# The head of a two-layer kernel: the first four weight chunks arrive in nine transfers of whole rows, and the idle matmuls at the start are lengthened

## The chip, the core and the metric

The kernel runs on one core of a Trainium2 chip. The metric is device time in microseconds for one execution, the median over the runs. A separate execution was recorded by the hardware profiler; all readings of single instructions, waits and transfers are from that one.

## The reference

Eight batches of 256 tokens with 1024 features pass two layers, each with a residual:

```python
# layer 0: per batch b a mask of zeros and ones and one number coeff[b]
sign = 2 * mask - 1
x = x + x @ W0.T + b0 + coeff[b] * (x @ sign[b])
# layer 1: a dense weight and a low-rank adapter chosen by itok[b]
x = x + x @ W1.T + b1 + 2.0 * ((x @ A[itok[b]]) @ B[itok[b]])
```

All of it is in float32, the mask is int32. In the first layer the weight of batch b is W0.T + coeff[b] * (2 * mask[b] - 1), so each batch has a weight of its own, made on the chip from a mask of 4 MB.

## The kernel before

Features lie on the 128 partitions; tokens run along the free dimension. Batch 0 goes through its weight in eight chunks of 128 input features by 1024 outputs (`first_batch`, L300); batches 1 and 2 in pieces of 256 inputs by 512 outputs (`first_layer`, L269); batches 3 to 7 use a scheme with seven instead of eight block products (class `Seven`, L335). After four batches the second layer of that group follows, also with seven products at two levels (`second_layer`, L702). Then the other four batches run the same way.

A piece of weight is made in two steps (`build`, L228). ScalarE turns the int32 mask into 2c * mask - c in float32 (L243; c is the batch's coefficient, held in `two_c` and `neg_c`). VectorE adds W0 to it (L251). TensorE then multiplies (L309 for batch 0, L284 for batches 1 and 2). One float32 matmul instruction of 256 columns appears as two passes in the records. From piece 8 on the identity has been added to W0 once (L236), which gives the residual; in batch 0 it is added while the sums leave PSUM (L322).

Loads are issued on SyncE's queue (SP) in the order of the pieces, four ahead of the piece that TensorE is at (`load`, L179; `load_to`). A transfer is issued when its buffer is free and the semaphore it uses has been served by its earlier user; eight such semaphores go round. W0 stays in one tile, `w0_sb`, for all batches; its chunks arrive with batch 0. For the first four chunks mask and W0 come in halves of 128x512 (256 KB each, L203), stored so that a half is contiguous in memory: mask half, W0 half, mask half, W0 half. The very first half is converted in two quarters of 256 outputs (`parts`, L152). x of chunk 0 is issued by ScalarE's queue (L205), x of chunk 1 by SP (L207), x of chunks 2 and 3 by SP (L209).

At the start, while the first bytes are on the way, TensorE multiplies zeros into a bank that nobody reads (`idle`, L98): 256 columns, then the little matmul `c_ps` that spreads the eight coefficients over the partitions (L106, it waits for the row of coefficients), then 256, 256 and 128 columns. VectorE makes `two_c` and `neg_c` from `c_ps` (L110, L112).

The order of instructions on each engine is made by a scheduler from the order of the program; `behind(...)` and `issue_after` pin some of them after others. The functions that the diff touches:

Of the kernel before, what the change touches and what calls it, by code (L numbers as in the profile page):

```python
# [9 lines left out]
F32 = mybir.dt.float32  # L10
I32 = mybir.dt.int32
AF = mybir.ActivationFunctionType
ALU = mybir.AluOpType

P = 128
OH = 512
CG = 2
OQ = 256
BY_HALF = 4
SEVEN = (3, 4, 5, 6, 7)  # L20
SCALING = 2.0

# [2 lines left out]
def kernel(  # L25
# [10 lines left out]
    b1: bass.AP,  # L36
    lora_a: bass.AP,
    lora_b: bass.AP,
    outT: bass.AP,
):  # L40

# [22 lines left out]
    nc = tc.nc  # L64
    B, NG, _, _, T = xT.shape
# [32 lines left out]
    def idle(*columns: int):  # L98
        for n in columns:
            nc.tensor.matmul(  # L100
                idle_ps[:, :n], lhsT=zeros[:, :P], rhs=zeros[:, :n], start=True, stop=True
            )

    idle(T)
    c_ps = psum.tile([P, B], F32, tag="ps", name="c_ps")
    spread = nc.tensor.matmul(c_ps, lhsT=one_row, rhs=c_row, start=True, stop=True)  # L106
    with tc.issue_after(spread.ins):
        idle(T, T, T // 2)
    two_c = const.tile([P, B], F32, tag="two_c", name="two_c")
    nc.vector.tensor_scalar_mul(two_c, c_ps, 2.0)  # L110
    neg_c = const.tile([P, B], F32, tag="neg_c", name="neg_c")
# [27 lines left out]
    anchors = {}  # L139
# [6 lines left out]
    def behind(what: str):  # L146
        return tc.issue_after(anchors[what].ins) if what in anchors else nullcontext()

    def pair(name):
        return qpool.tile([P, 2, CG, OQ], F32, tag="q", name=name)  # L150

    def parts(k: int):  # L152

        every = slice(0, OH)
        if k == 0:
            quarters = [(slice(0, 1), slice(q * OQ, (q + 1) * OQ)) for q in range(2)]
            return quarters + [(slice(1, 2), every)]
        return [(slice(i, i + 1), every) for i in range(2)] if k < BY_HALF else [(slice(0, 2), every)]

    def part(a, i: int):  # L160

        flat = a.rearrange("p i f -> (p i f)")
        return flat.rearrange("(i p f) -> i p f", i=2, p=P)[i]
# [15 lines left out]
    def load(k: int):  # L179

        b, h, g = pieces[k]

        if b in SEVEN and k % (2 * NG) >= 6 and b >= GB:
            pool, tag = qpool, "q"
        elif b in SEVEN and b % 2 and k % (2 * NG) < 6:
            pool, tag = tpool, "T"
        else:
            pool, tag = wpool, "w"  # L190
        weff[k] = pool.tile([P, CG, OH], F32, tag=tag, name=f"w_{k}")
        last = (k + 1) % (GB * 2 * NG) == 0
        pairs = [(weff[k].bitcast(I32), mask[b, g if b == 0 else h * NG + g])]
        if b == 0:
            pairs.append((w0_of(k), w0T[g]))
        x_pair = g // CG if b == 0 and g % CG == 0 else g if h == 0 else None
        if x_pair is not None:
            x = x_sb[b, x_pair] = xpool.tile([P, CG, T], F32, tag=f"x{x_pair}", name=f"x_{b}_{x_pair}")
        if k < BY_HALF:

            for i in range(2):
                for t, a in pairs:
                    nc.sync.dma_start(t[:, i], part(a, i))  # L203
                if k == 0 and i == 0:
# [12 lines left out]
        if k == NG:  # L217
            nc.sync.dma_start(b0_sb, b0)
        if k == 2 * NG:
            nc.sync.dma_start(itok_sb, itok)  # L220
        for n, (q, r) in enumerate(W1_ORDER):
            if k == 0 and r % 2 == 0:
                two = pair(f"w1_{q}_{r // 2}")
                raw[q, r], raw[q, r + 1] = two[:, 0], two[:, 1]
            if k == 2 * NG + 2 * n // 3:
                nc.sync.dma_start(raw[q, r], w1T[q, r])

    def build(k: int):  # L228
# [8 lines left out]
        w = weff[k]  # L237
        m = w.bitcast(I32)
        for i, o in parts(k):


            with behind("bias"):
                nc.scalar.activation(  # L243
                    w[:, i, o],
                    m[:, i, o],
                    AF.Identity,
                    bias=neg_c[:, b : b + 1],
                    scale=two_c[:, b : b + 1],
                )
            with behind("adds"):  # L250
                weff_at[k] = nc.vector.tensor_add(w[:, i, o], w[:, i, o], w0_of(k)[:, i, o])  # L251
            anchors["weights"] = weff_at[k]

    loaded = 0

# [44 lines left out]
    def first_batch(y, beside):  # L300

        ps = [bank(f"ps1_0_{i}") for i in range(NC // 2)]
        for c in range(NC):
            load_to(c + LOADS_AHEAD + 1)
            build(c + BUILDS_AHEAD)
            w = weff.pop(c)
            for ot in range(NC):
                h, j = divmod(ot, TPH)
                nc.tensor.matmul(  # L309
                    ps[ot // 2][:, ot % 2, :],  # L310
                    lhsT=w[:, h, j * P : (j + 1) * P],
                    rhs=x_sb[0, c // CG][:, c % CG, :],
                    start=c == 0 and ot % 2 == 0,
                    stop=c == NC - 1,
                    skip_group_check=True,
                )
# [826 lines left out]
```

## Time and profile before

| | us |
|---|---|
| median of 3 runs | 407.4 (407.25 to 407.57) |
| the profiled execution's own time | 407.66 |
| its span, first to last instruction | 406.0 |
| TensorE busy in the span | 401.6 |
| VectorE busy | 314.2 |
| ScalarE busy | 137.1 |
| first mask half landed | 3.52 |
| first W0 half landed | 4.74 |
| first matmul of batch 0 | 5.35 |
| first matmul of batch 1 | 34.83 |
| first matmul of batch 3 | 90.09 |

All times inside the profile count from the span's start. PE is TensorE's matmuls and PEld its weight loads, DVE VectorE, ACT ScalarE, POOL GpSimd, SP SyncE. The slices of the page cut the span into 40 equal parts of 10.15 us; a digit is the busy share in tenths. In a row of stretches the numbers are the stretch, its length, busy time and (in brackets) instructions of each engine, the granted clock, the share of the DMA engines and GB/s. A line of the chain of waits is start, duration and what ran. A row of the timeline is start, duration, engine, line of the kernel, instruction, its tiles and shapes, how many, and in square brackets the idle time before it with what ended it. A matmul's record is longer than the distance to the next one, since matmuls overlap; their rate is read from the distance between starts.

### The profile page before, as it was taken

How to read it: one execution, taken by the hardware profiler on the slowest of the kernel's cores; microseconds unless marked ns; L12 is line 12 of the kernel's file. 1: busy time of each engine (PE TensorE's matmuls, PEld its weight loads, DVE VectorE, ACT ScalarE, POOL GpSimd, SP SyncE). 2: the span in 40 equal slices, each digit the busy share in tenths (PEclk: the TensorE clock that was granted, in tenths of full speed). 3: DMA queues.
4: the chain of work that ended last, by engine and by line, in shares of the span. 5: the costliest groups of instructions: out<-in, count | busy, mean ns of one | idle time of the engine just before them, and what ended most of it. 6: DMA issues, size and time to landing. Idle time of an engine off the chain costs nothing.

```text
span 406.0 us, 6808 instructions
## 1 busy us (share of the span) xinstructions
PE 401.6 (99%) x2562; PEld 360.0 (89%) x2562; DVE 314.2 (77%) x451; ACT 137.1 (34%) x223; POOL 52.5 (13%) x103
## 2 busy tenths in 40 slices
PE   8999999999999999999999999999999999999997
PEld 6888888889977888888899999999998788888886
DVE  2447696979992779987999999999926247898595
ACT  4444535673114213132141927528221420102200
POOL 0000143004944221011040000400000000000000
PEclk9999999999999999999999999999999999999999
DMA  8999999990699799766998947631022237555654
GB/s 286 399 403 396 401 409 417 391 366 5 215 364 353 243 342 320 237 231 210 313 383 317 345 148 289 223 109 54 27 79 68 78 127 241 170 152 155 212 173 158
DMA packets 41700, 99.56 MB, mean 245 GB/s; under 512 B 5700, under 2 KB 6340, under 8 KB 41668
## 3 DMA queue, kind: packets, MB, share of 16 engines
q1 hardware_dynamic: 32978, 76.11, 53.8%
q0 software_dynamic: 6240, 18.90, 12.3%
q10 hardware_dynamic: 2450, 4.13, 2.8%
q8 instruction: 20, 0.33, 0.3%
q14 instruction: 12, 0.10, 0.1%
HBM read 79.19 MB, written 19.92 MB: 244 GB/s over the span
## 4 chain that ended last, share of the span: by engine, by line
PE 90%; DVE 7%; DMA 1%; ACT 1%; issue 0%; SPq 0%; DVEq 0%; ACTq 0%
PE X L727 23%; PE ps L284 14%; PE X L427 13%; PE Z L727 12%; PE ps L309 7%; PE Z L427 6%; PE Y L727 6%; PE Y L427 4%; DVE w L251 3%; PE G L745 2%; DVE s L363 2%; PE psh L762 2%; DVE t L380 1%; PE W L868 1%; DMA w_sb<-w0T 1%; DVE y L453 1%
## 5 line engine op out<-in xcount | busy, mean ns | idle before, releaser
L243 ACT ACTIVATE w<-w,neg_c,two_c 128x1024 f32<-128x1024 int32 (+2 forms) x69 | 79.1, 1183 | 60.4 <-DMA w<-mask 50.4
L251 DVE TENSOR_TENSOR w<-w,w_sb 128x1024 f32<-128x1024 f32 (+2 forms) x69 | 77.7, 1142 | 27.0 <-ACT w L243 19.8
L284 PE MATMUL ps<-x,w 128*128 128x256 f32 x256 | 55.4, 379 | 0.0
L284 PEld LDWEIGHTS ps<-x,w 128*128 128x128 f32 x256 | 48.6, 190 | 6.6
L446 ACT ACTIVATE y<-X,b_sb 128x128 f32<-128x128 f32 x60 | 17.2, 368 | 69.9 <-PE X L427 69.9
L427 PE MATMUL X<-t,s 128*128 128x128 f32 x288 | 34.1, 276 | 0.0
L883 DVE TENSOR_TENSOR c<-c,e 128x512 f32<-128x512 f32 x48 | 31.8, 682 | 1.8 <-ACT c L755 1.8
L427 PEld LDWEIGHTS X<-t,s 128*128 128x128 f32 x288 | 33.0, 192 | 0.2
L309 PE MATMUL ps<-x,w 128*128 128x256 f32 x128 | 29.5, 394 | 0.2 <-DVE w L251 0.2
L755 ACT COPY c<-G 128x512 f32<-128x512 f32 x32 | 16.4, 600 | 38.8 <-PE G L745 38.8
L309 PEld LDWEIGHTS ps<-x,w 128*128 128x128 f32 x128 | 25.3, 199 | 4.2 <-DVE w L251 0.5
L783 ACT COPY e<-X 128x512 f32<-128x512 f32 x16 | 9.4, 587 | 48.6 <-PE X L727 48.6
L785 DVE TENSOR_TENSOR c<-X,c 128x512 f32<-128x512 f32 x24 | 16.3, 686 | 8.9 <-PE X L727 8.7
L427 PE MATMUL X<-t,w 128*128 128x128 f32 x192 | 22.5, 276 | 0.4 <-DVE y L453 0.4
L727 PE MATMUL X<-T_t,l_S_s 128*128 128x256 f32 x96 | 22.7, 379 | 0.0
L427 PEld LDWEIGHTS X<-t,w 128*128 128x128 f32 x192 | 21.9, 192 | 0.5 <-DVE y L453 0.5
L363 DVE TENSOR_TENSOR s<-w,w 128x1024 f32<-128x1024 f32 x18 | 21.7, 1217 | 0.1
L727 PEld LDWEIGHTS X<-T_t,l_S_s 128*128 128x128 f32 x96 | 18.2, 190 | 2.5
L785 DVE TENSOR_TENSOR e<-Y,e 128x512 f32<-128x512 f32 x8 | 5.5, 691 | 17.6 <-PE Y L727 17.6
L427 PE MATMUL Z<-t,s 128*128 128x128 f32 x160 | 18.8, 275 | 0.0
L427 PE MATMUL X<-x,w 128*128 128x128 f32 x160 | 18.8, 275 | 0.0
L427 PE MATMUL Y<-x,w 128*128 128x128 f32 x160 | 18.7, 275 | 0.0
(145 smaller groups left out, 672.0 us busy)
## 6 DMA issues: line engine op xcount, KB each, us to landing
w<-mask SPq DMA_DIRECT2D x60, 512.0 KB, 7.0
l_S_s<-leaf_S_s SPq DMA_DIRECT2D x32, 256.0 KB, 2.7
x<-xT SPq DMA_DIRECT2D x31, 256.0 KB, 6.6
l_A_s<-leaf_A_s SPq DMA_DIRECT2D x24, 256.0 KB, 2.8
l_S_a<-leaf_S_a SPq DMA_DIRECT2D x24, 256.0 KB, 3.2
w<-w1T SPq DMA_DIRECT2D x16, 256.0 KB, 7.2
outT<-c POOLq DMA_DIRECT2D x15, 256.0 KB, 5.5
outT<-c ACTq DMA_DIRECT2D x15, 256.0 KB, 2.4
```

The costliest lines, as they stand in the source:

```text
L243: nc.scalar.activation(w[:, i, o], m[:, i, o], AF.Identity, bias=neg_c[:, b : b + 1], scale=two_c[:, b : b + 1],)
L251: weff_at[k] = nc.vector.tensor_add(w[:, i, o], w[:, i, o], w0_of(k)[:, i, o])
L284: nc.tensor.matmul(ps[j // 2][:, j % 2, :], lhsT=w[:, c, j * P : (j + 1) * P], rhs=x_sb[b, g][:, c, :],  start=first and j % 2 == 0, stop= ...
L309: nc.tensor.matmul(ps[ot // 2][:, ot % 2, :], lhsT=w[:, h, j * P : (j + 1) * P], rhs=x_sb[0, c // CG][:, c % CG, :], start=c == 0 and ot % ...
L363: anchors["weights"] = anchors["sums"] = op(s, self.w[x, a], self.w[y, a])
L427: anchors["products"] = nc.tensor.matmul(ps[:, j, :], lhsT=w[:, c, j * P : (j + 1) * P], rhs=r, start=first and a == 0 and c == 0 and j == ...
L446: sent = nc.scalar.activation(self.out(i, v)[:, j, :], ps[:, j, :], AF.Identity, bias=b0_sb[:, ot : ot + 1])
L727: anchors["inner"] = nc.tensor.matmul(ps[:, j, :], lhsT=l[:, c, j * P : (j + 1) * P], rhs=r[:, c, :], start=first and c == 0 and j == 0, s ...
L755: nc.scalar.copy(dest[b // 2][u, b % 2], ps[b])
L783: anchors["copies"] = nc.scalar.copy(out, ps)
L785: own["reads"] = anchors["reads"] = nc.vector.tensor_add(out, ps, other)
L883: nc.vector.tensor_add(o, o, x)
```

## The change

Three things change together.

First, for chunks 0 to 3 of batch 0, mask and W0 no longer come as separate transfers into their tiles. The host lays out a new array `head`: for each of nine parts, a row per feature that holds the mask's outputs, then W0's outputs, and in the first part also x of chunk 0 (256 tokens). The parts are outputs 0 to 256, 256 to 512 and 512 to 1024 of chunk 0, and two halves of each of chunks 1, 2 and 3. Each part is one transfer, a row of 3 KB (first), 2 KB (second) or 4 KB (the rest) for each partition, into a tile borrowed from buffers that are used later: the tiles T, t and q. x of chunk 0 is read from there; ScalarE's queue no longer issues it.

Second, for these chunks ScalarE reads the mask from the head tile and writes into the weight tile, and VectorE adds W0 from the head tile. W0 reaches `w0_sb` later: ScalarE copies it there (nine copies, `put_w0`), the copies of chunk c placed behind the conversion of piece c + 4.

Third, zeros on TensorE: 128 more columns ahead of `c_ps` and 64 more at the end.

```diff
-BY_HALF = 4
+HEAD = [(0, 0, 256, True), (0, 256, 512, False), (0, 512, 1024, False)]
+HEAD += [(c, h * OH, (h + 1) * OH, False) for c in range(1, 4) for h in range(2)]
+N_HEAD = 4
...
-    idle(T)
+    idle(T, T // 2)
...
-        idle(T, T, T // 2)
+        idle(T, T, T // 2, T // 4)
...
+    in_head = {}
+    row = 0
+    for c, a, e, with_x in HEAD:
+        n = 2 * (e - a) + (T if with_x else 0)
+        if n > 2 * OQ:
+            pool, tag = (tpool, "T") if c + 1 < N_HEAD else (qpool, "q")
+        else:
+            pool, tag = spool, "t"
+        t = pool.tile([P, n], I32, tag=tag, name=f"head_{c}_{a}")
+        in_head.setdefault(c, []).append((a, e, t, head[row * P : (row + n) * P]))
+        row += n
+
     def parts(k: int):
...
+        if k not in in_head:
+            return [(weff[k], weff[k].bitcast(I32), w0_of(k))]
+        w = weff[k].rearrange("p i o -> p (i o)")
+        return [
+            (w[:, a:e], t[:, : e - a], t[:, e - a : 2 * (e - a)].bitcast(F32))
+            for a, e, t, _ in in_head[k]
+        ]
+
+    def x_of(c: int):
+
+        if c:
+            return x_sb[0, c // CG][:, c % CG, :]
+        return in_head[0][0][2][:, -T:].bitcast(F32)
+
+    def put_w0(c: int):
+
+        for a, e, t, _ in in_head[c]:
+            nc.scalar.copy(w0_sb[:, c, a:e], t[:, e - a : 2 * (e - a)].bitcast(F32))
...
-        if k < BY_HALF:
-
-            for i in range(2):
-                for t, a in pairs:
-                    nc.sync.dma_start(t[:, i], part(a, i))
-                if k == 0 and i == 0:
-                    nc.scalar.dma_start(x[:, 0], part(xT[0, 0], 0))
-                elif k == 0:
-                    nc.sync.dma_start(x[:, 1], part(xT[0, 0], 1))
-                elif x_pair is not None and i == 0:
-                    nc.sync.dma_start(x, xT[b, x_pair])
+        if k in in_head:
+            for _, _, t, at in in_head[k]:
+                nc.sync.dma_start(t, at.rearrange("(p f) -> p f", p=P))
+            if k == 0:
+                nc.sync.dma_start(x[:, 1], xT[0, 0][:, 1])
+            elif x_pair is not None:
+                nc.sync.dma_start(x, xT[b, x_pair])
...
-            with behind("bias"):
-                nc.scalar.activation(
-                    w[:, i, o],
-                    m[:, i, o],
-                    AF.Identity,
-                    bias=neg_c[:, b : b + 1],
-                    scale=two_c[:, b : b + 1],
+            with behind("bias" if b else "first"):
+                anchors["first"] = nc.scalar.activation(
+                    w, m, AF.Identity, bias=neg_c[:, b : b + 1], scale=two_c[:, b : b + 1]
                 )
             with behind("adds"):
-                weff_at[k] = nc.vector.tensor_add(w[:, i, o], w[:, i, o], w0_of(k)[:, i, o])
+                weff_at[k] = nc.vector.tensor_add(w, w, w0)
             anchors["weights"] = weff_at[k]
+        if N_HEAD <= k < 2 * N_HEAD:
+            with behind("first"):
+                put_w0(k - N_HEAD)
...
-                    rhs=x_sb[0, c // CG][:, c % CG, :],
+                    rhs=x_of(c),
...
-                    x_sb[0, ot // CG][:, ot % CG, :],
+                    x_of(ot),
```

x of chunks 2 and 3 is now issued behind both halves of chunk 2, where it stood between them. The conversions of batch 0 are pinned in their order, each after the one before.

More of the change, by code (lines that the diff above doesn't have):

```diff
@@ L38 @@
     lora_b: bass.AP,
+    head: bass.AP,
     outT: bass.AP,
@@ L150, in pair @@
         return qpool.tile([P, 2, CG, OQ], F32, tag="q", name=name)
-    def parts(k: int):
[L154 to L163, printed above, removed]
+    in_head = {}
[9 more added lines that the diff above has]
+        row += n
+    def parts(k: int):
+        if k not in in_head:
[12 more added lines that the diff above has]
+            nc.scalar.copy(w0_sb[:, c, a:e], t[:, e - a : 2 * (e - a)].bitcast(F32))
     def w0_of(k: int):
@@ L236, in build @@
                     nc.vector.tensor_add(d, d, ident)
-        w = weff[k]
-        m = w.bitcast(I32)
-        for i, o in parts(k):
-            with behind("bias"):
-                nc.scalar.activation(
-                    w[:, i, o],
-                    m[:, i, o],
-                    AF.Identity,
-                    bias=neg_c[:, b : b + 1],
-                    scale=two_c[:, b : b + 1],
+        for w, m, w0 in parts(k):
+            with behind("bias" if b else "first"):
+                anchors["first"] = nc.scalar.activation(
+                    w, m, AF.Identity, bias=neg_c[:, b : b + 1], scale=two_c[:, b : b + 1]
                 )
             with behind("adds"):
-                weff_at[k] = nc.vector.tensor_add(w[:, i, o], w[:, i, o], w0_of(k)[:, i, o])
+                weff_at[k] = nc.vector.tensor_add(w, w, w0)
             anchors["weights"] = weff_at[k]
+        if N_HEAD <= k < 2 * N_HEAD:
+            with behind("first"):
+                put_w0(k - N_HEAD)
     loaded = 0
@@ L1121 @@
     }
-    def by_part(a):
-        a[:] = np.moveaxis(a, 1, 0).reshape(a.shape)
     arrays["mask"][0] = np.asarray(mask_Bx4096x4096_ik1)[0].reshape(D // P, P, 2, OH)
-    for k in range(BY_HALF):
-        by_part(arrays["mask"][0, k])
-        by_part(arrays["w0T"][k])
-    by_part(arrays["xT"][0, 0])
+    w0T, x0 = np.asarray(L0_cond_W).T, x[0].T
+    rows = []
+    for c, a, e, with_x in HEAD:
+        i = slice(c * P, (c + 1) * P)
+        row = [np.asarray(mask_Bx4096x4096_ik1)[0, i, a:e], laid(w0T[i, a:e]).view(np.int32)]
+        if with_x:
+            row.append(laid(x0[i]).view(np.int32))
+        rows.append(np.concatenate(row, axis=1).reshape(-1))
+    arrays["head"] = np.concatenate(rows)
     nc = bacc.Bacc("TRN2", target_bir_lowering=False, num_devices=1)
```

## The prediction

> **What bounds the kernel now.** I read the page first: engine shares and slices.
>
> ```profile
> PE 401.6 (99%) x2562; PEld 360.0 (89%) x2562; DVE 314.2 (77%) x451; ACT 137.1 (34%) x223; POOL 52.5 (13%) x103
> PE   8999999999999999999999999999999999999997
> DMA  8999999990699799766998947631022237555654
> GB/s 286 399 403 396 401 409 417 391 366 5 215 364 353 243 342 320 237 231 210 313 383 317 345 148 289 223 109 54 27 79 68 78 127 241 170 152 155 212 173 158
> ```
>
> TensorE is busy everywhere but at the two ends, and for the first 90 us (nine slices) the DMA engines are full as well, near 400 GB/s. So two things can pace that stage. Next, the chain of waits in order of time:
>
> ```profile
> 1.31 3.43 DMA w_sb<-w0T
> 4.87 0.43 DVE w L251
> 5.35 29.48 PE ps L309 x128
> 34.83 55.25 PE ps L284 x256
> 90.09 3.57 PE X L427 x32
> 93.66 3.57 PE Y L427 x32
> 97.23 3.73 PE X L427 x32
> ```
>
> Until 5.35 us the kernel waits for W0's first half; from there TensorE runs without a break. But 128 matmul passes in 29.48 us are slow: 256 like passes take 55.25 us (216 ns each), so 128 should take 27.6. Busy time in stretches of 2 us shows where the 1.85 us are:
>
> ```profile
> 4.00:6.00 2.00, 1.82 (x6) 1.26 (x6) 0.76 (x2) 1.18 (x3) 0.00 (x0) 1.00 0.91 324
> 6.00:8.00 2.00, 2.00 (x6) 1.60 (x5) 0.69 (x1) 0.37 (x2) 0.00 (x0) 1.00 1.05 394
> 8.00:10.00 2.00, 2.00 (x9) 1.67 (x8) 0.69 (x1) 1.48 (x2) 0.00 (x0) 1.00 1.04 376
> 10.00:12.00 2.00, 2.00 (x11) 1.75 (x10) 1.19 (x2) 0.93 (x2) 0.00 (x0) 1.00 1.03 394
> ```
>
> The third number is TensorE's, its records in brackets. In the records passes start 427 ns apart up to 8.50 us and 216 ns apart afterwards, and the trace's clock record begins full speed at 8.60 us. The first eight passes are at half speed.
>
> The last row of the chain holds 3.73 us where its neighbours hold 3.57. The timeline says why:
>
> ```profile
> 86.61 5.17 ACT L243 ACTIVATE w<-w,neg_c,two_c 128x1024 f32<-128x1024 int32 x4 [0.71 <-DMA w<-mask]
> 87.89 2.50 DVE L251 TENSOR_TENSOR w<-w,w_sb 128x1024 f32<-128x1024 f32 x2 [0.72 <-ACT w L243]
> 97.63 1.22 DVE L363 TENSOR_TENSOR s<-s,w 128x1024 f32<-128x1024 f32 x1
> ```
>
> ScalarE waits for a mask of batch 3 until 86.61; VectorE then works without idle from 87.89 to 98.85, and the matmuls that read this sum go on at 98.91, 0.06 us late. TensorE thus has no slack there against a chain that starts with a landing of the full DMA stream. Starting TensorE earlier pays only as far as that landing moves too.
>
> [...]full speed lasts from 8.60 to 407.96 us, 399.36 us[...]. [...]W0's second half lands on its engines between 5.65 and 6.94, fifteen of them by 6.32. [...]x of chunk 0 from ScalarE's queue shares those engines; its 128 packets lie among SP's from 3.2 to 4.3 us.
>
> **The change, part by part.**
>
> *Zeros.* Before, zeros stream to 1.89, the coefficient row arrives, its spread streams at 2.32, zeros again 2.84 to 4.97, and the first real pass, its weights loaded from 5.35, streams at 5.52. The added 128 columns (two passes of 213 ns) run 1.89 to 2.31, just up to the spread, so two_c and neg_c stay at 2.78 and 2.86. The added 64 columns (two of 107 ns) run 4.97 to 5.18. [...]
>
> *First transfer.* Packets of 1, 2 and 4 KB take 46, 84 and 159 ns, so 3 KB takes some 121 (estimate). Each engine carries 8 rows: 8 x 121 = 0.97 us where the first mask took 0.67 and landed at 3.52. So mask, W0 and x land together at 3.82; before, W0 was there at 4.74 and x at 4.94. Then ScalarE 0.59, VectorE 0.42 and 0.2 of hand-overs: weights at 5.03. The zeros end at 5.18; real passes stream from there, 0.33 earlier than before, weights loaded beneath the last zeros.
>
> *What mask and W0 in one row costs.* Before, ScalarE converted a mask while its W0 was still in flight; now both steps follow the landing: 0.02 + 0.81 + 0.04 + 0.69 + 0.05 = 1.61 us (the times of chunk 1 before) where W0's landing was followed by 0.88. At full clock the first two quarters need 8 x 216 ns, to 6.93. The second quarter (landing about 4.5) is ready by 5.6, in time. The third transfer, 1152 KB into the stream, is nominally there at 5.8; the same byte was there at 6.94 before, with one engine 0.62 behind the rest. I take 6.0, so ready at 7.6 (7.4 to 8.5). TensorE idles 0.7 us, and begins the second half of chunk 0 at 7.6 instead of 8.77: 1.15 us ahead. Chunk 1 follows with 1.33 us per half against 1.73 on TensorE; x of chunks 2 and 3 (landed at 13.34, needed at 12.8) and chunk 4 (weights 0.94 us ahead before) are tight unless the stream moves too.
>
> *DMA stream.* 256 KB in rows of 2 KB took 0.667 us per landing, 512 KB in rows of 4 KB 1.28. Seven transfers of 512 KB save 7 x 0.054 = 0.38 us, the first two and x 0.07 (1.71 against 1.64 on an engine). The engines also lost about 0.75 us by 8 us (1928 KB where full rate would have moved them by 7.0), half of it at 4.2 to 5.8, and the slowest 0.6 more. With ScalarE's transfer gone and twice the bytes behind each issue I take 0.3 of that back, bounds 0 and 0.8. Sum 0.75 us (0.45 to 1.25). Total bytes are unchanged. SP's issues fall from 18 to 11 for these chunks; at 0.33 to 0.47 us each they aren't what the engines wait for later.
>
> *W0 put in place.* Nine copies on ScalarE, 0.6 us for 512 columns (its 128x512 COPY row, from PSUM there), 0.4 for 256: 5.0 us between 18 and 30 us, 1.2 to 1.4 behind each conversion of chunks 4 to 7. ScalarE's idle times there are 2.07, 1.39, 2.63 and 1.33 us, so they fit; without that cover a conversion comes up to 0.1 late, where weights stand 1 us ahead of TensorE. VectorE's additions of the identity wait for the last copy, at about 30; their readers start at 34.8. The buffers that the head borrows are next wanted after 50 us. Two ScalarE conversions of chunks around batch 3 swap places, and VectorE takes them in the same order as before. All nothing.
>
> *Sum.* TensorE comes 1.15 us earlier to the point at 98.9, the landing behind VectorE's chain 0.75: the smaller counts. Later stages follow from TensorE's own results. Profiled execution: 407.66 (span 406.0 and 1.66 around it) - 0.75 = 406.9. It was 0.26 above the median of the runs, so 406.65.
>
> **Rivals.**
>
> *More (406.2).* The engine that fell 0.62 behind doesn't, and the stream gains 1.2. For: one packet of 608 ns at 4.74 stands alone. Against: such stalls may strike anywhere.
>
> *The stream is no faster (407.2).* Larger rows save bus time, but landings are set by the slowest engine; at 80 to 90 us it trails the first by 2 us, and the head's saving can drown in that. Then TensorE arrives early and waits at 98.9; 0.0 to 0.4 is left, 407.2. The early start is then hidden anyway.
>
> *The clock isn't raised earlier (407.2).* [...]Real passes then start 0.33 earlier at half clock, eight of them end at 8.6, 0.17 ahead of before, plus the 0.06 of the wait at 98.9: 0.23.
>
> *Slower (408.8).* TensorE's new idle time between 6.93 and the third transfer's weights is its own danger. [...]1.8 us lost, start equivalent to 10.2 against 8.77, 1.4 later, all of it on the path.[...]
>
> **How the numbers follow.** Main case 0.45 at 406.65 (406.3 to 406.9); more 0.17; no faster stream 0.14; clock as before 0.12; slower 0.12. 0.2% (about what a measurement here can tell from no change) is 0.81 us, so under 406.6: half of the main case and "more", 0.40. Over 408.2: 0.12. Between: 0.48. The range runs from a stream gain of 1.6 (the bounds of rows and losses, and some of the slow engine's) to the hidden cases with the spread of runs: 405.8 to 407.7, with the slower case left out.
>
> **What would show it.** Passes 216 ns apart from the first real one; first conversion at about 3.9, first pass near 5.2; a hole in TensorE from 6.9 to 7.6; the mask wait at 86.61 moved to about 85.9; a wait for VectorE of some 0.4 us inside the row at 97.23. It is wrong if passes stay at 427 ns to 8.6, if they return to it after 8.6, or if that mask wait hasn't moved or moved by more than 1.3.

## The result and the profile after

The kernel after takes 407.83 us (median of 22 runs, 407.48 to 408.25); the kernel before took 407.25 us in the same session (22 runs, 406.79 to 407.92). The ratio is 1.0015, 95% interval 1.0009 to 1.0022. So it is a little slower, by some 0.6 us, where 406.65 was forecast, some 0.75 us faster; 407.83 lies above the range of 405.8 to 407.7. The change is small, but its interval leaves out 1, and it has the other sign than forecast. The two profiled executions differ by less than the medians do (407.83 after, 407.66 before); why one pair is a weak measure here comes out of the experiments.

The page of the kernel after, first the engines' shares, then TensorE and the DMA engines in 40 slices:

```profile
PE 401.7 (99%) x2566; PEld 360.6 (89%) x2566; DVE 314.1 (77%) x451; ACT 141.7 (35%) x232; POOL 52.6 (13%) x103
PE   8999999999999999999999999999999999999997
...
DMA  7999999990699799776898947631122247545654
GB/s 272 407 403 396 395 406 417 413 360 4 223 365 337 250 335 318 244 231 217 296 372 338 345 148 278 235 111 52 27 78 57 80 140 233 170 153 161 211 167 160
```

ScalarE has 4.6 us more work, the nine copies. The first slice, up to 10.15 us, moved 272 GB/s where it was 286 before. That is 0.14 MB less in just the stretch that the change was to speed up. In the second slice the stream is a little faster (407 against 399); from the third to the seventh the two are within 5 GB/s.

The longest pieces of the chain of waits, in order of time, start and duration (the conversion and addition between the first two rows are left out):

```profile
1.78 5.59 DMA head<-head
...
8.99 26.17 PE ps L328 x120
35.16 55.25 PE ps L303 x256
...
93.98 3.57 PE Y L446 x32
97.55 3.57 PE X L446 x32
```

Before, the chain began with W0's first half and TensorE had no break after 5.35 us. Now its first long piece is the third transfer, issued at 1.78 and landed at 7.37, and the first eight passes have dropped off the chain: the 120 passes after them are what counts, and these begin at 8.99, 1.62 us after the landing. They run at full speed (218 ns each) and bring batch 1 to 35.16, where it began at 34.83. The row at 97.55 no longer holds a wait for VectorE.

The stretches of 2 us, columns as before (the third number is TensorE, in brackets its records; the last two are the DMA engines' share and GB/s):

```profile
4.00:6.00 2.00, 2.00 (x8) 1.82 (x7) 0.85 (x2) 1.11 (x2) 0.00 (x0) 1.00 0.82 255
6.00:8.00 2.00, 2.00 (x6) 1.55 (x6) 0.00 (x0) 0.61 (x1) 0.00 (x0) 1.00 0.95 341
8.00:10.00 2.00, 1.67 (x9) 1.14 (x8) 0.82 (x2) 1.03 (x2) 0.00 (x0) 1.00 1.03 420
10.00:12.00 2.00, 2.00 (x11) 1.76 (x10) 1.25 (x2) 1.23 (x2) 0.00 (x0) 1.00 1.01 410
```

Two things stand in the last column. From 4 to 8 us the engines moved 255 and 341 GB/s, against 324 and 394 before; from 8 us on they moved 420 and 410, against 376 and 394. The loss comes first, in the stretch that decides when the second half of chunk 0 is there; the gain comes behind it.

The timeline of the start (start, duration, engine, line, instruction, tiles, in square brackets the idle time before it and what ended it):

```profile
3.90 0.60 ACT L263 ACTIVATE w<-head,neg_c,two_c 128x256 f32<-128x256 int32 x1 [0.99 <-DMA head<-head]
...
4.54 0.43 DVE L267 TENSOR_TENSOR w<-w,head 128x256 f32<-128x256 f32 x1 [1.22 <-ACT w L263]
4.74 0.60 ACT L263 ACTIVATE w<-head,neg_c,two_c 128x256 f32<-128x256 int32 x1 [0.24 <-DMA head<-head]
...
5.58 3.08 PE L328 MATMUL ps<-head,w 128*128 128x256 f32 x8
...
7.39 0.82 ACT L263 ACTIVATE w<-head,neg_c,two_c 128x512 f32<-128x512 int32 x1 [2.05 <-DMA head<-head]
...
8.24 0.69 DVE L267 TENSOR_TENSOR w<-w,head 128x512 f32<-128x512 f32 x1 [2.44 <-ACT w L263]
...
8.99 1.35 PE L328 MATMUL ps<-head,w 128*128 128x256 f32 x5 [0.33 <-DVE w L267]
```

The first weights stand at 4.97, 0.33 us ahead of before (5.30). TensorE is still at its zeros and takes its first real pass at 5.58, where it took it at 5.35. Then ScalarE waits 2.05 us for the third part, VectorE 2.44 for ScalarE, and TensorE gets the second half of chunk 0 at 8.99.

At batch 3, the same view:

```profile
86.41 5.09 ACT L263 ACTIVATE w<-w,neg_c,two_c 128x1024 f32<-128x1024 int32 x4 [0.71 <-DMA w<-mask]
87.68 2.44 DVE L267 TENSOR_TENSOR w<-w,w_sb 128x1024 f32<-128x1024 f32 x2 [0.73 <-ACT w L263]
...
97.37 1.23 DVE L382 TENSOR_TENSOR s<-s,w 128x1024 f32<-128x1024 f32 x1
97.39 3.74 PE L446 MATMUL X<-t,s 128*128 128x128 f32 x32
```

The mask that was there at 86.61 is there at 86.41: the whole stream gained 0.20 us. VectorE's sum ends at 98.60, where it ended at 98.85. TensorE comes to that point later than before (the block begins at 97.39, in the kernel before at 97.07), so it finds the sum ready. That hides half of the loss in this pair: batch 1 begins 0.33 us later than before, the row at 97.55 is 0.16 us shorter than its counterpart, and the two executions differ by 0.17 us.

### The profile page after: what moved, and what is told of

It reads as the page before. It is cut to its first block, busy times and chain, and to the rows that moved or that the text cites. A ratio compares the mean times of both kernels' runs of the same rounds, so it can differ in the third digit from the quotient of the medians.

```text
span 406.1 us, 6825 instructions
## 1 busy us (share of the span) xinstructions
PE 401.7 (99%) x2566; PEld 360.6 (89%) x2566; DVE 314.1 (77%) x451; ACT 141.7 (35%) x232; POOL 52.6 (13%) x103
## 4 chain that ended last, share of the span: by engine, by line
PE 89%; DVE 7%; DMA 1%; ACT 1%; issue 0%; SPq 0%; DVEq 0%; ACTq 0%
PE X L746 23%; PE ps L303 14%; PE X L446 13%; PE Z L746 12%; PE ps L328 6%; PE Z L446 6%; PE Y L746 6%; PE Y L446 4%; DVE w L267 3%; PE G L764 2%; DVE s L382 2%; PE psh L781 2%; DMA head<-head 1%; DVE t L399 1%; PE W L887 1%; DVE y L472 1%
## 5 line engine op out<-in xcount | busy, mean ns | idle before, releaser
L263 ACT ACTIVATE w<-w,neg_c,two_c 128x1024 f32<-128x1024 int32 x60 | 72.5, 1248 | 49.4 <-DMA w<-mask 44.3
L267 DVE TENSOR_TENSOR w<-w,w_sb 128x1024 f32<-128x1024 f32 x60 | 72.1, 1220 | 18.0 <-ACT w L263 14.7
L303 PE MATMUL ps<-x,w 128*128 128x256 f32 x256 | 55.4, 379 | 0.0
L303 PEld LDWEIGHTS ps<-x,w 128*128 128x128 f32 x256 | 48.6, 190 | 6.6
L328 PE MATMUL ps<-x,w 128*128 128x256 f32 x112 | 24.3, 379 | 0.0
L328 PEld LDWEIGHTS ps<-x,w 128*128 128x128 f32 x112 | 21.3, 190 | 2.9
```

What stands on the lines that cost most here:

```text
L263: anchors["first"] = nc.scalar.activation(w, m, AF.Identity, bias=neg_c[:, b : b + 1], scale=two_c[:, b : b + 1])
L267: weff_at[k] = nc.vector.tensor_add(w, w, w0)
L303: nc.tensor.matmul(ps[j // 2][:, j % 2, :], lhsT=w[:, c, j * P : (j + 1) * P], rhs=x_sb[b, g][:, c, :],  start=first and j % 2 == 0, stop= ...
L328: nc.tensor.matmul(ps[ot // 2][:, ot % 2, :], lhsT=w[:, h, j * P : (j + 1) * P], rhs=x_of(c), start=c == 0 and ot % 2 == 0, stop=c == NC - ...
```

## The experiments

My theory after the result: **supply**. The second half of chunk 0 and chunk 1 come later than before, since the stream of the head is slower in the first 8 us and since ScalarE must wait for mask and W0 both; that pins TensorE near 9 us whenever its clock would have let it be there earlier. Rivals: the new **zeros** delay the coefficients and the first pass; the **copies** on ScalarE hold something up; a **clock** that falls back in the hole.

All times are medians; the kernel before stood at 407.3 us in every session (407.25 to 407.32). Each ratio is to the kernel before. Each profile is one execution, which may lie well off its kernel's median.

### Zeros alone, and the change without its zeros

The kernel before with the two new zeros:

```diff
-    idle(T)
+    idle(T, T // 2)
...
-        idle(T, T, T // 2)
+        idle(T, T, T // 2, T // 4)
```

> The kernel before with the longer zeros alone. If the late third transfer is what costs (supply), the zeros are harmless or help: two_c and neg_c come 0.3 us later, still ahead of the first mask at 3.5; [...]TensorE then waits only for the second half's weights (ready at 7.8 in the profile before): 0.0 to 0.5 us faster than before. If the zeros themselves cost (they push the first real pass, or the coefficients), 0.3 to 0.6 us slower, as much as the whole change.

Measured: 407.07 us, ratio 0.9993 (0.9986 to 0.9999). The zeros cost nothing; they may have won a little. This is the lowest median of all kernels here and the only one whose interval lies below 1.

The kernel after with the zeros of before (the same edit backwards):

> The changed kernel with the zeros of before. Supply: the second half of chunk 0 is still ready only near 8.9, so the time stays within 0.2 us of the changed kernel (0.4 to 0.7 slower than before). Zeros at fault: back to before, within 0.2 us.

Measured: 407.83 us, ratio 1.0014 (1.0005 to 1.0023), just as with the new zeros. Its profiled execution had the clock at full speed from 6.23 us on, the earliest so far, and didn't profit from it. The timeline:

```profile
5.16 2.51 PE L328 MATMUL ps<-head,w 128*128 128x256 f32 x8
7.42 0.82 ACT L263 ACTIVATE w<-head,neg_c,two_c 128x512 f32<-128x512 int32 x1 [2.25 <-DMA head<-head]
8.27 0.69 DVE L267 TENSOR_TENSOR w<-w,head 128x512 f32<-128x512 f32 x1 [2.64 <-ACT w L263]
9.02 1.16 PEld L328 LDWEIGHTS ps<-head,w 128*128 128x128 f32 x6 [1.75 <-DVE w L267]
```

The eight passes began 0.42 us earlier than in the kernel after and were half of the time at full speed, and yet the second half of chunk 0 begins at 9.02 against 8.99. What went ahead of it has been waited away: the weight loads stood still for 1.75 us. So zeros neither cause the loss nor can they cure it. Nor did the clock fall back in the hole: TensorE was idle for 1.35 us ahead of 9.02, and the 120 passes from there took 26.17 us, 218 ns each.

### Other transfers

The kernel after, with each part of 512 outputs sent as two transfers, first the mask's half of the row, then W0's:

```diff
-                nc.sync.dma_start(t, at.rearrange("(p f) -> p f", p=P))
+                rows = at.rearrange("(p f) -> p f", p=P)
+                cut = t.shape[1] // 2 if t.shape[1] == 2 * OH else t.shape[1]
+                nc.sync.dma_start(t[:, :cut], rows[:, :cut])
+                if cut < t.shape[1]:
+                    nc.sync.dma_start(t[:, cut:], rows[:, cut:])
```

> The changed kernel, but every part of 512 outputs is sent as two transfers, mask then W0, cut from the same rows, so that conversion need not wait for W0. Supply by waiting for both: the second half is ready 0.7 us earlier after the same last byte (landing + 0.88 instead of + 1.61), TensorE begins it at 8.2 to 8.5 instead of 8.99: 0.4 to 0.6 us faster than the changed kernel. Supply by late bytes alone (the third transfer's last byte at 7.4): only as far as rows of 2 KB land earlier, 0 to 0.2. Copies or buffers at fault: no change against the changed kernel.

Measured: 407.53 us, ratio 1.0002 (0.9992 to 1.0011).

The kernel after with chunks 0 and 1 in quarters of 256 outputs:

```diff
-HEAD = [(0, 0, 256, True), (0, 256, 512, False), (0, 512, 1024, False)]
-HEAD += [(c, h * OH, (h + 1) * OH, False) for c in range(1, 4) for h in range(2)]
+HEAD = [(c, q * OQ, (q + 1) * OQ, c + q == 0) for c in range(2) for q in range(4)]
+HEAD += [(c, h * OH, (h + 1) * OH, False) for c in range(2, 4) for h in range(2)]
```

> The changed kernel with chunks 0 and 1 in quarters of 256 outputs (rows of 2 KB, of 3 KB for the first), eight transfers for them instead of five. Supply: the first quarter of the second half lands at about 6.1 and is ready at 7.3, so TensorE goes on without a hole: 0.4 to 0.8 us faster than the changed kernel, level with before or 0.3 faster. Copies, buffers or zeros at fault: no change.

Measured: 407.30 us, ratio 1.0001 (0.9993 to 1.0009). By the medians the first brings about half of the 0.6 us back (0.30 us, between the two cases of its expectation) and the second all of it, while copies, zeros, the pinned order of the conversions and the head itself stay. In their timelines the second half of chunk 0 is ready when its last addition ends, at 7.50 and 7.40 instead of 8.93. (That TensorE has no hole in these two profiles says little: its passes were at half speed to about 9 us in both, so it asked late.) That speaks for supply. How much of it is the separate landing and how much the smaller rows these two don't separate.

Then only the third part in two, which by a narrow reading of the chain should have been enough:

```diff
-(0, 512, 1024, False)]
+(0, 512, 768, False), (0, 768, 1024, False)]
```

> The kernel after, with one part changed: the third (outputs 512 to 1024 of chunk 0) comes as two parts of 256 outputs. If this one transfer's late landing is the loss, the first of the two lands by about 5.9, TensorE has no hole at 8.3, and the time is 407.2 to 407.4 as with quarters for chunks 0 and 1 (407.30). If chunk 1's halves of 4 KB rows, which land at 8.99 and 10.27, would hold TensorE up next, about half of the gain is left: 407.5 to 407.7, with a hole near 10.5.

Measured: 408.03 us, ratio 1.0019 (1.0011 to 1.0027). By this time nothing came back, and both of my cases failed. But the time of this kernel can't be set beside the others as it stands, since some 0.8 us of it lie outside the work. VectorE's last sum ends at 403.30 in its profile and at 403.60 in that of the kernel after, yet the executions took 408.31 and 407.83 us, which leaves 5.0 us against 4.2. Half of the 0.8 is in the records: at the end SyncE waits for the semaphores one after the other, 0.06 us apart, and with one transfer more than in the kernel after the last output's comes third (404.89) instead of last, so that seven more follow it. The other half lies outside the span: 2.0 to 2.1 us in all its 21 runs where every other kernel has 1.6 to 1.8; why is open. Without the 0.8 us the median would be near 407.25 (an estimate; the half inside the span is from the one profile), the first of the two cases: most of the loss came back. (In the same way 0.3 us of the profile with quarters in two chunks stand at its end.) The profiled execution, 407.5 us without them, is one of the slower ones, and its timeline shows what can be left:

```profile
6.51 1.27 ACT L263 ACTIVATE w<-head,neg_c,two_c 128x256 f32<-128x256 int32 x2 [1.13 <-DMA head<-head]
...
8.81 0.81 ACT L263 ACTIVATE w<-head,neg_c,two_c 128x512 f32<-128x512 int32 x1 [1.03 <-DMA head<-head]
9.66 0.69 DVE L267 TENSOR_TENSOR w<-w,head 128x512 f32<-128x512 f32 x1 [1.42 <-ACT w L263]
...
10.40 0.73 PEld L328 LDWEIGHTS ps<-x,w 128*128 128x128 f32 x4 [1.19 <-DVE w L267]
```

The second half of chunk 0 now begins at 7.66, as the prediction had it, but chunk 1's first half lands at 8.79 and TensorE stands again until 10.40. Counted back by the 1.73 us of a half, that is a start at 8.67. The chain's first row named one late transfer; behind it, in this execution, stood a second that was nearly as late. By the estimate above it came sooner in most of the others.

### Where the parts lie, and how much of the head is needed

The kernel after with its nine parts 4 MB apart in memory:

```diff
-    row = 0
-    for c, a, e, with_x in HEAD:
+    for part_no, (c, a, e, with_x) in enumerate(HEAD):
+        row = part_no * APART
```

> The kernel after, with the nine parts of the head array 4 MB apart in memory instead of back to back; every transfer and its row sizes as after. If the slow packets of the first 9 us (0.3 to 1.1 us for 4 KB where 0.16 is usual) come from all transfers reading one stretch of memory, the third part lands near 6.0 us instead of 7.37, the hole in TensorE goes, and the time falls to about 407.2. If they come with the large rows or the order of the transfers, whatever their place, the third part lands at 7.2 to 7.5 again and the time stays at 407.7 to 407.9.

Measured: 407.84 us, ratio 1.0015 (1.0007 to 1.0023), like the kernel after. In its one profile the third part landed at 6.63 rather than 7.37, but chunk 1's first half at 8.94 (8.99 after), and TensorE had holes ahead of both, the second up to 10.56. The chain of waits begins with the second:

```profile
2.72 6.22 DMA head<-head
10.56 24.44 PE ps L328 x112
35.00 55.25 PE ps L303 x256
```

So an earlier third part alone won 0.16 us at the start of batch 1, since chunk 1's first half came as late as in the kernel after: here it isn't one transfer, it is the stream. The distance between the parts doesn't matter to the time.

Only the first half of chunk 0 and x in the head, the rest as in the kernel before (mask and W0 separate, rows of 2 KB), zeros as after, two copies instead of nine:

```diff
-HEAD = [(0, 0, 256, True), (0, 256, 512, False), (0, 512, 1024, False)]
-HEAD += [(c, h * OH, (h + 1) * OH, False) for c in range(1, 4) for h in range(2)]
+HEAD = [(0, 0, 256, True), (0, 256, 512, False)]
+BY_HALF = 4
```

> The kernel after, with only the first two parts (first half of chunk 0, and x) in the head; the second half of chunk 0 and chunks 1 to 3 come as before, mask and W0 as separate transfers of 2 KB rows from their own arrays, and only the two quarters of W0 are copied by ScalarE. Supply theory: the early first pass and the new zeros stay, the second half of chunk 0 is converted as soon as its mask is there (about 6.0) and its weights stand by 7.5, so nothing is lost: 406.8 to 407.2, no slower than the kernel before with the new zeros alone (407.07). If it is the merged first part itself, or the lost queue of ScalarE, that costs, it comes out at 407.5 or more.

Measured: 407.21 us, ratio 1.0002 (0.9994 to 1.0010): the loss is gone, but at a hundredth above the range that I had named it isn't shown to be faster than before either, and the early first part has won nothing over the zeros alone. Its profile is the counterpart to the second experiment, an execution in which the clock was full early, from 6.77 us. The chain of waits:

```profile
5.79 28.23 PE ps L339 x128
34.02 55.25 PE ps L314 x256
```

No hole: TensorE turns the early clock into a start of batch 1 at 34.02, and the execution took 406.96 us, the lowest of its 13 runs.

### Copies alone

The kernel before, with nine copies at the places where the change puts W0 in place (here W0 onto itself):

```diff
+        if 4 <= k < 8:
+            for a, e in ((0, 256), (256, 512), (512, 1024)) if k == 4 else ((0, 512), (512, 1024)):
+                with behind("first"):
+                    nc.scalar.copy(w0_sb[:, k - 4, a:e], w0_sb[:, k - 4, a:e])
```

> The kernel before, with nine copies on ScalarE at the places where the change puts W0 in place (here each copies a piece of W0 onto itself). My step counted them at nothing: 407.1 to 407.4, within 0.05% of before. Rival: the copies hold up conversions of chunks 4 to 8 and with them TensorE, or slow VectorE's additions that run beside them: 407.6 or more, with a later start of batch 1 than 34.85 to 35.0.

Measured: 407.31 us, ratio 1.0000 (0.9990 to 1.0010). The copies are free. Its timeline shows them and the wait that hides them:

```profile
17.19 1.24 ACT L243 ACTIVATE w<-w,neg_c,two_c 128x1024 f32<-128x1024 int32 x1 [1.14 <-DMA w<-mask]
18.34 1.22 ACT L256 COPY w_sb<-w_sb 128x256 f32<-128x256 f32 x3
20.50 1.24 ACT L243 ACTIVATE w<-w,neg_c,two_c 128x1024 f32<-128x1024 int32 x1 [0.95 <-DMA w<-mask]
```

ScalarE waits for a mask anyway, 0.95 us even behind three copies. Batch 1 starts at 36.26 in this profile, which the expectation had named as the rival's sign, but this is the slowest of the 13 executions (408.95 us) and its clock was full only from 10.93; the last table below has the same late start without any copies. The rival of the copies falls.

### Row size or source

By 7.4 us packets of 1 KB and more had brought, in KB by the records of the transfers (one profiled execution each):

| kernel | rows from the head | other rows of mask and W0 | KB by 7.4 us |
|---|---|---|---|
| before; zeros alone; copies alone; before without zeros (below) | none | 2 KB | 1782; 1838; 1718; 1736 |
| first half of chunk 0 only | 3 and 2 KB | 2 KB | 1696 |
| quarters in two chunks | 2 KB, then 4 KB | none so far | 1666 |
| two transfers | 2 KB | none so far | 1618 |
| third part in two | 2 KB, 4 KB from chunk 1 on | none so far | 1588 |
| after; old zeros; parts apart; after without zeros (below) | 4 KB from the third on | none so far | 1508; 1535; 1500; 1481 |

The kernel after is 274 KB behind the kernel before, 0.7 us at 400 GB/s. Packets that took longer than usual make up the difference: what they took beyond the usual 46, 84, 121 and 159 ns for 1 to 4 KB comes to 1.1 us for each of the 16 engines after and to 0.4 before. Only half of the 1.1 is in packets of 4 KB, and packets that took 1 us and more stand in kernels with 2 KB rows too (1.2 us with quarters in two chunks). Two more kernels separate what the table mixes. First, the kernel before with whole chunks of 4 KB rows from its own arrays:

```diff
-BY_HALF = 4
+BY_HALF = 0
```

> The kernel before with mask and W0 of all eight chunks as whole transfers of 512 KB in rows of 4 KB (chunk 0's mask and W0 and x of chunks 0 and 1 too), from their own arrays. Only what has landed by 7.4 us is of interest: 1782 to 1858 KB in kernels with rows of 2 KB from these arrays, 1500 to 1535 KB in those with rows of 4 KB from the head. If rows of 4 KB are what slows the stream early on, it has 1400 to 1600 KB by 7.4 us; if it is the one array that is read, 1700 or more. The time is longer whatever the answer, since the first weights wait for a whole chunk: 408.5 to 410.

Measured: 1760 KB by 7.4 us, where the comparable kernels have 1718 to 1838 (the 1858 in the expectation should read 1838). The time is 409.79 us, ratio 1.0074 (1.0049 to 1.0100), since the first weights wait for a whole chunk. Large rows as such are not slow, and x of chunk 0 came on SyncE's queue here too, so it isn't the second queue that the stream misses. Second, the kernel after with all four chunks in quarters, so that all rows of the head but the first are 2 KB:

```diff
-HEAD = [(0, 0, 256, True), (0, 256, 512, False), (0, 512, 1024, False)]
-HEAD += [(c, h * OH, (h + 1) * OH, False) for c in range(1, 4) for h in range(2)]
+HEAD = [(c, q * OQ, (q + 1) * OQ, c + q == 0) for c in range(4) for q in range(4)]
```

> The kernel after with all four chunks of the head in quarters of 256 outputs: sixteen transfers, all rows 2 KB but the first (two quarters share a tile in chunks 2 and 3). If the size of the rows is what slows the stream, it has 1700 KB or more by 7.4 us, the weights of the second half of chunk 0 and of chunk 1 come in time, and the time is 406.9 to 407.3. If it is the head array, 1600 to 1670 KB as with quarters in two chunks, and 407.3 to 407.6.

Measured: 1656 KB by 7.4 us, and 407.54 us, ratio 1.0002 (0.9994 to 1.0011), both in the ranges of the second case. So the head costs some stream with rows of either size, and more with 4 KB, by one profile of each kernel. Why is open: it may be the array, or the tiles that the rows land in, which differ from those of before as well; no run separates these two. The quarters don't lead to a gain, as the chain of waits shows:

```profile
5.79 7.93 PE ps L333 x32
13.75 20.96 PE ps L333 x96
```

Chunks 0 and 1 go through without a stop from 5.79, and TensorE then waits up to 13.75 for a quarter of chunk 2.

### Two attempts at more, and no zeros at all

Since zeros alone did best, I took away what breaks them (that an unbroken row of zeros would bring full speed earlier was an estimate of mine): the coefficients come to all partitions by a transfer of 128 rows of 32 bytes, and no matmul spreads them. On top of the kernel before:

```diff
-    nc.scalar.dma_start(c_row, coeff)
+    nc.scalar.dma_start(c_all, bass.AP(tensor=coeff.tensor, offset=coeff.offset, ap=[[0, P], [1, B]]))
...
-    idle(T)
-    c_ps = psum.tile([P, B], F32, tag="ps", name="c_ps")
-    spread = nc.tensor.matmul(c_ps, lhsT=one_row, rhs=c_row, start=True, stop=True)
-    with tc.issue_after(spread.ins):
-        idle(T, T, T // 2)
+    idle(T, T, T, T, T)
```

> The kernel before, with the eight coefficients brought to all 128 partitions by the transfer itself (128 rows of 32 bytes on ScalarE's queue, no matmul that spreads them), and five zeros of 256 columns without a hole from 0.9 us. [...]its supply allows a start of chunk 0's second half near 7.6. I expect 406.7 to 407.0 (before 407.3) and a narrower spread. Rival: the coefficients land late or the transfer pushes the first mask back; then the first pass comes at 5.6 or later and the time is 407.2 or more.

And the same edit on top of the kernel with only the first half of chunk 0 in the head:

> As the run above (coefficients by the transfer, five zeros without a hole), on top of the kernel in which only the first half of chunk 0 and x come in the head. Weights of the first pass stand at 4.96 instead of 5.3, but the zeros end near 5.3 in both unless the clock has risen, so it should be within 0.2 us of the run above: 406.6 to 407.0. If the stream of the head is what costs, it is slower than the run above by 0.3 or more.

Measured: 408.77 us, ratio 1.0037 (1.0025 to 1.0048), and 409.53 us, ratio 1.0047 (1.0031 to 1.0064). The rival came true in both. Timeline of the first:

```profile
0.86 0.41 ACTq L90 DMA_DIRECT2D c_all<-coeff  x1
...
5.18 0.17 DVE L106 TENSOR_SCALAR two_c<-c_all 128x8 f32<-128x8 f32 x1 [4.07 <-DMA c_all<-coeff]
...
5.46 1.09 ACT L239 ACTIVATE w<-w,neg_c,two_c 128x256 f32<-128x256 int32 x2 [2.17 <-DVE neg_c L108]
...
6.80 1.38 PEld L305 LDWEIGHTS ps<-x,w 128*128 128x128 f32 x7 [2.02 <-DVE w L247]
```

The 4 KB of coefficients, issued at 0.86, are there at 5.15; the first conversion waits for them, and the first mask, too, lands at 4.98 where it landed at 3.52. The 128 packets occupy an engine for only 7 to 9 ns each, but they lie spread from 2.51 to 4.63 us. In the trace they and the rows of 2 KB from the other queue take turns on an engine, one row at a time.

Last, both kernels without any zeros, to see whether the loss depends on an early clock (that full speed would come later without them was an estimate of mine):

```diff
-    idle(T, T // 2)
...
-    with tc.issue_after(spread.ins):
-        idle(T, T, T // 2, T // 4)
```

> The kernel after without any zeros on TensorE. [...]eight or more passes run at half speed: supply has time. If supply that binds only under an early clock is what makes the kernel after slower, then here it isn't: 408.1 to 408.6, and 0.0 to 0.5 us faster than the kernel before without zeros, since its first pass comes earlier. Rival: if the rows or the copies cost something whatever the clock, it stays 0.4 us or more slower than the kernel before without zeros.

> The kernel before without any zeros on TensorE, as the partner of the run above. [...]408.2 to 408.8.

Measured: 408.33 us, ratio 1.0023 (1.0012 to 1.0034), and 408.15 us, ratio 1.0010 (0.9995 to 1.0025). The difference is 0.18 us instead of 0.58, but after stays the slower one, and the intervals overlap. Neither my expectation (0.0 to 0.5 faster) nor the rival (0.4 or more slower) was met; this pair decides nothing. One part of it was plainly wrong: eight or more passes at half speed were to give the supply its time, but in the profile of after without zeros the clock was full from 8.02, ahead of the eighth pass (8.17), and the hole was there again: the ninth starts at 9.33.

### What the profiled executions say together

Full speed comes at another time in every profiled execution, from 6.18 to 11.24 us in the table. Ordered by that moment, with the start of batch 1 and the landing that TensorE waited for, from the chain of waits:

| second half of chunk 0 and chunk 1 | full clock from | landing waited for | batch 1 starts |
|---|---|---|---|
| as before: first half of chunk 0 only in the head | 6.77 | none | 34.02 |
| as before: the kernel before | 8.60 | none behind the first weights | 34.83 |
| as before: copies alone | 10.93 | none behind the first weights | 36.26 |
| as before: without zeros | 11.24 | none behind the first weights | 36.11 |
| head, 4 KB rows: third part in two | 6.18 | 8.79, chunk 1 | 34.85 |
| head, 4 KB rows: old zeros | 6.23 | 7.40, third part | 35.19 |
| head, 4 KB rows: parts apart | 6.92 | 8.94, chunk 1 | 35.00 |
| head, 4 KB rows: after | 7.87 | 7.37, third part | 35.16 |
| head, 4 KB rows: after without zeros | 8.02 | 7.71, third part | 35.50 |

With the loads of before, batch 1 follows the clock, some half microsecond per microsecond, as it must where passes at half speed are what is lost. (The last two stand in the other order, since their first passes are 0.6 us apart.) With the head it follows the landing: in all five the passes go on 1.61 or 1.62 us behind it and run at full speed from there, 120 of them behind the third part, 112 behind chunk 1, and an earlier clock brings nothing. The pair of profiles that the result began with is one of a late clock (before) and an earlier one (after); at the same clock the difference would be larger. All quarters lie between the two groups (7.62, 34.71). Three profiles (zeros alone, two transfers, quarters in two chunks) have no clock record; by the distance of their passes full speed came near 9.1, and batch 1 starts at 35.16, 35.16 and 35.26 there. The two kernels without the spread are left out, since their first weights come late.

The runs without a profile agree. The lowest of the kernel before was 406.79 us in the first session and 406.45 to 406.82 in the others; the lowest of after, old zeros, parts apart and after without zeros were 407.48, 407.48, 407.48 and 407.49, in 14 to 22 runs each. The head takes away the fast executions, as it must if an early clock no longer helps.

## Why the prediction was wrong

**The mechanism of supply failed, at one step: the landing of the third transfer.** "I take 6.0, so ready at 7.6 (7.4 to 8.5)" measured 7.37 and 8.93. The working behind it was sound as far as it went: from the landing to the first pass it took 1.62 us (1.61 predicted), the first transfer landed at 3.81 (3.82), its weights stood at 4.97 (5.03). What was wrong is the stream. I took 0.3 of the 0.75 us back that the engines had lost by 8 us; instead they were 0.7 us further behind by 7.4 us. The bounds I gave, 0 and 0.8, left out a loss, and nothing in the profile excluded it: that is the error in the method. Why the stream came later stays open, as said above. With a landing at 7.4, the step's own sum gives 9.0, later than the 8.77 of before.

**The second error is that only the first such point was priced.** The profiles with the third part in two and with the parts apart show that chunk 1's first half, at 8.79 and 8.94 and with 1.6 us of serial work, can hold TensorE at the same place. The prediction had "1.33 us per half against 1.73", so chunk 1 follows easily; it does, if it doesn't land late.

**Stream at batch 3:** 0.75 predicted, 0.20 measured at the mask wait of 86.61. Behind the loss the stream caught up: 274 KB behind the kernel before at 7.4 us, 128 at 12 and 60 at 20, at 420 and 410 GB/s against 376 and 394 from 8 to 12. Whether that is the rows' saving no run shows; it mostly pays for the loss before it. "Wrong if that mask wait hasn't moved" was nearly the case. The rule "the smaller counts" at 98.9 could not be seen at work, since TensorE came late and waited for nothing there.

**Zeros:** the time of two_c was to stay at 2.78; it moved to 3.08, since the weights of the little matmul were loaded at 2.45 rather than 2.15. That cost nothing, the first part landed later still. The zeros ran on until the first pass at 5.58, 0.2 after the first pass before (5.35) instead of 0.3 ahead of it; the early weights at 4.97 weren't used. By the runs with old and new zeros (1.0014 against 1.0015 with the head, 0.9993 without it) this is no part of the loss.

**Clock:** that TensorE would be at full speed from its first real pass was my estimate; what decides when full speed comes, no trace here shows. In the profile after, passes start 427 ns apart from 6.12 to 7.82 and 216 ns apart from 8.06, and the clock record begins full speed at 7.87. Since that moment lies anywhere from 6.18 to 11.24 us in the profiles above, 7.87 rather than 8.60 isn't shown to be the change's doing, nor can the rival "the clock isn't raised earlier" be judged by one profile.

**Copies:** nothing predicted, ratio 1.0000 measured.

**Rivals:** "more" fell. "The stream is no faster" came nearest: the loss is one of landings; but it put them at batch 3 and priced it at a small gain. "Slower" had the right place, the idle time ahead of the third part's weights, and the wrong payment: that the clock may fall back there was my estimate, and it did not in any profiled execution of the kernels with the head's 4 KB rows. In the kernel after the pass ahead of the hole starts at 8.28, the one behind it at 8.99, and the 120 from there take 26.17 us, as with the old zeros behind 1.35 us without a pass. What was paid is the hole itself. Without a fall of the clock the loss was 0.2 us in the two profiles and 0.6 by the medians, not 1.4, and I had no case for it: the gap between "no faster" and "slower" is where the result fell.

**Two more readings that were off.** x of chunks 2 and 3 landed at 11.97 in the kernel before, not at 13.34, so it was not tight; and by the ends of the packets 2012 KB had come by 8 us, not 1928. Nothing in the result hangs on them.

## What to carry to other kernels

Merging two inputs into one transfer makes the first of two serial steps wait for the last byte of both: price every part behind the first by its own landing, with a loss of stream among the bounds, until the consumer has slack again. When a wait is removed or moved, look for the next one right behind it at the same place (here chunk 1 behind the third part) before taking the gain. When a time moves the wrong way, look at the end of the execution too: one more transfer at the start went with 0.8 us more outside the work. Where full speed comes at another time in every execution (6.18 to 11.24 us here), compare several or sort them by that moment; the 22 runs of the kernel before alone spread over 1.1 us, twice what was to be explained.

## What was unexpected in the hardware

The moment of full speed differs by 5 us between executions (6.18 with the third part in two, 11.24 in the kernel before without zeros); what decides it isn't shown. With the old zeros it was not lost in a hole: TensorE ran no pass for 1.35 us ahead of 9.02, and the passes from there are 218 ns apart. In the second attempt without the spread it was lost, at 7.75 by that profile's clock record. At the end of the run it outlasted the last pass: in the kernel before that pass starts at 402.84 and full speed ends at 407.96; in the kernel after, 403.00 and 407.23. In both it had lasted 399.36 us, though it began at 8.60 and at 7.87.

The first 8 us of the stream depend on more than bytes and row size: 1760 KB by 7.4 us in 4 KB rows from the arrays of before, 1481 to 1535 KB in 4 KB rows from the head. Single packets of 4 KB took up to 1.11 us there in the kernel after (159 ns is usual), packets of 2 KB up to 0.61 us in the kernel before (84 ns). From 8 to 12 us the same kind of transfer moved 420 and 410 GB/s in the kernel after, where it had moved 255 from 4 to 6. A broadcast of 32 bytes to 128 partitions took 4.3 us from issue (0.86) to use (5.18) at the start of the kernel before without the spread.
